# Who begins the transfer of the carried rows: ScalarE's queue in place of SyncE's

## The chip, the core and the metric

The kernel runs on one NeuronCore of a Trainium2 chip. The time is that of the device, in microseconds, for one execution of the whole program, and the median over several runs is compared. The names of the engines are those of the profile: PE is TensorE's matmul, PEld its weight load, DVE is VectorE, ACT is ScalarE, POOL is GpSimd and SP is SyncE, which only begins transfers. A `q` behind a name (SPq, ACTq) means the engine's instruction queue, which waits and begins transfers and in which the engine itself does no arithmetic.

## The reference

The input x has 32 batches of 512 channels by 1024 nodes, and adj is a 512 by 512 matrix. Layer 0 is a graph attention over the nodes, layer 1 a linear map with adj * adj, each behind a layer norm and a relu, and each added to x:

```
h = max(layernorm(x), 0)
q = wq . h ; k = wk . h                      # one number a node
scores[m, n] = leaky(q[n] + k[m], 0.01)
x = x + relu(adj @ (h @ softmax(scores).T) + bm)
h = max(layernorm(x), 0)
x = x + (adj * adj).T @ h + bias
```

## The kernel before

All is float32. The 1024 by 1024 scores are never formed. The leaky function has two slopes, so exp(score) is one product of exponentials where q[n] + k[m] is positive and another where it isn't. If the nodes are sorted by q, each output node needs one sum over an upper part of the sorted list and one over a lower part. So a batch goes through these steps, each a small function of the kernel:

- `load`, `stats`, `norm`, `slopes`, `relu` (layer 0): x comes in, ACT and DVE normalise it. `scores` (PE, then an ACT copy at L380 and a small transfer at L381 on ACT's queue) and `row` (L386, also on ACT's queue) spread q over all partitions.
- `rank` (DVE) and `lower` (ACT, L433) count for each node how many q are smaller. `value` (PE, L474) multiplies h with adj; `spread` (ACT, L481) copies each result out of its bank of PSUM; `scatter` (POOL, L487) writes the rows, sorted, into a table in DRAM (`td`).
- `fetch` (SP, L503) brings the sorted table back in three tiles `vs` of three blocks. `weights` (ACT, L510 to L515) makes the exponentials; `later` (DVE, L523 and L527) and `totals` prepare the weights and denominators; `stationary` (POOL, L546) multiplies masks with weights.
- `scan` and `sums` make the running sums over the nine blocks, once from each end. `scan` i multiplies block 8 - i into the upper 64 rows of a bank and block i into the lower 64 rows. `sums` i copies the bank out to a tile `t` (ACT, L574), puts the denominators beside it (ACT, L578) and has SP write both halves into the table (L580, L581).
- The sum so far has to enter the next block. In each block of 128 rows, row 0 or row 64 is kept free for it, so `sums` i carries the last sums, one row of 512 numbers for each direction, into the tiles `vs` that `scan` i + 1 reads. In batches 5 to 27 the rows go from `t` by two transfers of 2 KB (L576, L577); in the first five and last four batches ACT copies them straight from PSUM (L572, L573). The ninth block has nothing to carry.
- `gather` (POOL, L586) fetches for each node its sums, `excess`, `divide`, `weigh` (ACT, L611) and `combine` (DVE, L615) mix them, `turn` (PE and DVE, L622 and L626) transposes and adds to x.
- Layer 1: norm again, then seven products in place of eight on half-sized blocks. `seed` has ACT put the bias into banks (L648), `propagate` (PE, L657) multiplies, `mix` (DVE, L644) makes sums of blocks of h, `finish` (DVE, L670 and L674) adds to x, and `store` (SP, L701) writes out.

The order of all these steps, over several batches that are in work at once, is written out by hand in a long string, `ORDER`; every step is put into the queues of its engines in that order. There is no scheduler at run time: each engine goes through its own queue in order, and a waiting instruction holds up all that stands behind it in the same queue. `tp` has two buffers for `t`, `vsp` five for `vs`, and PSUM has eight banks that all steps share. Each transfer that SP or ACT begins counts on one of eight completion counters, taken in turn; before a transfer may use its counter, the one before on that counter must have landed.

Of the kernel before, what the change touches and what calls it, by code (L numbers as in the profile page):

```python
# [160 lines left out]
def kernel(  # L161
# [32 lines left out]
    nc = tc.nc  # L194
    B, C, N = x.shape
# [6 lines left out]
    HP = P // 2  # L202
# [364 lines left out]
    def sums(s, i):  # L567
        p = s.pt.pop(i)
        ha, hb = NB - 1 - i, i
        t = tp.tile([P, W], F32, tag="t", name=f"t_{s.b}_{i}")  # L570
        if i < NB - 1 and not LO <= s.b < B - HI:
            nc.scalar.copy(s.vs[ha - 1][0:1, 0:C], p[0:1, :])  # L572
            nc.scalar.copy(s.vs[hb + 1][HP : HP + 1, 0:C], p[HP : HP + 1, :])  # L573
        nc.scalar.copy(t[:, 0:C], p)  # L574
        if i < NB - 1 and LO <= s.b < B - HI:
            nc.sync.dma_start(s.vs[ha - 1][0:1, 0:C], t[0:1, 0:C])  # L576
            nc.sync.dma_start(s.vs[hb + 1][HP : HP + 1, 0:C], t[HP : HP + 1, 0:C])  # L577
        nc.scalar.copy(t[:, C:W], s.den[:, i : i + 1].broadcast_to([P, W - C]))  # L578
        td = tds[s.b % TABLES].rearrange("(s k) w -> s k w", k=4)
        nc.sync.dma_start(td[ts(ha, HP), 0, :], t[0:HP, :])  # L580
        nc.sync.dma_start(td[ts(hb, HP), 2, :], t[HP:P, :])  # L581
# [130 lines left out]
    for b in range(B):  # L712
        s = Batch()
# [8 lines left out]
        for f, count in (  # L722
            (rank, NN), (lower, NN), (value, NN), (spread, NN), (scatter, NN),
            (to_rows, 2), (scan, NB), (sums, NB), (gather, NN), (weigh, NN),
        ):
            plan(s, f, f.__name__, count=count)
# [30 lines left out]
    for code in ORDER.split():  # L757
        for k in range(0, len(code), 2):
# [3 lines left out]
            s, t = args[0], len(steps)  # L762
# [31 lines left out]
```

## Time and profile before

| | |
|---|---|
| median of 3 runs | 2300.36 us (2294.92 to 2301.21) |
| the profiled execution's own time | 2299.28 us |
| its span, first to last instruction | 2297.6 us |
| mean granted PE clock | 0.992 |
| busy: PE, DVE, ACT, POOL | 2225.3, 1735.6, 1703.1, 704.9 us |
| transfers begun at L576 and L577 | 184 and 184, on SP's queue, from 375.7 to 1974.8 us |
| one issue on SP, median | 539 ns at L576, 582 ns at L577 |
| one issue on ACT, median | 502 ns at L381, 341 ns at L386 |
| the two copies, mean | 581 ns at L574 (128 by 512), 207 ns (median) at L578 (128 by 16) |

All of it is one execution, recorded by the hardware. The busy time of an engine is the sum of its instructions; issues on a queue aren't counted in it. A line of the timeline has the start in us from the span's beginning, the length in us, the engine and the line of the kernel, the operation, what it writes and reads, the sizes and the count of instructions merged; in brackets at the end stand the idle time of the engine before it and what ended that. A line of the waits has who waited, for whom, the us in total, how often, and the longest.

### The profile page before, as it was taken

The numbers are of one execution on the slowest core, as the hardware profiler recorded it, in microseconds if no ns is written. First come the engines' busy times: TensorE is split into PE (matmuls) and PEld (weight loads), VectorE is DVE, ScalarE is ACT, GpSimd is POOL, SyncE is SP. The second block draws the span as 40 slices with busy tenths as digits, with TensorE's granted clock in tenths as the row PEclk, the third lists the DMA queues.
The fourth block names the chain that finished last, engine by engine and source line by source line (L and its number), as shares of the span: only waits on it lengthen the run. The fifth ranks groups of instructions, "written<-read, shape, count | busy, mean of one in ns | idle before, by whom it ended". The sixth has DMA issues, their size and how long they took to land. (4 is left out here: it accounts for less than half of the span.)

```text
span 2297.6 us, 28803 instructions
## 1 busy us (share of the span) xinstructions
PE 2225.3 (97%) x7344; PEld 954.0 (42%) x7344; DVE 1735.6 (76%) x4876; ACT 1703.1 (74%) x3269; POOL 704.9 (31%) x979
## 2 busy tenths in 40 slices
PE   6999999999999999999999999999999999999987
PEld 3434434344444444444444444444443444444343
DVE  6878878777877877777877877877777878778462
ACT  4698698777677877677877777877777876888752
POOL 2345223233232333232333232333222333234210
PEclk9999999999999999999999999999999999999998
DMA  6697887787888888888888888888888888788951
GB/s 234 225 341 258 310 290 294 276 298 266 314 284 303 299 314 282 291 281 314 295 316 290 300 275 304 309 302 294 300 275 293 301 310 277 283 283 314 368 220 73
DMA packets 217717, 657.77 MB, mean 286 GB/s; under 512 B 39376, under 2 KB 39504, under 8 KB 217552
## 3 DMA queue, kind: packets, MB, share of 16 engines
q1 hardware_dynamic: 153760, 362.16, 45.7%
q0 software_dynamic: 57344, 276.86, 31.4%
q10 hardware_dynamic: 6448, 16.92, 2.6%
q8 instruction: 59, 0.97, 0.2%
q14 instruction: 106, 0.87, 0.1%
HBM read 438.05 MB, written 217.01 MB: 285 GB/s over the span
## 5 line engine op out<-in xcount | busy, mean ns | idle before, releaser
L474 PE MATMUL pv<-wmT,x 128*128 128x512 f32 x2048 | 919.2, 598 | 0.7 <-ACT x L366 0.6
L474 PEld LDWEIGHTS pv<-wmT,x 128*128 128x128 f32 x2048 | 378.5, 190 | 496.5 <-issue 440.2
L487 POOL DMA_INDIRECT td<-v,idx x256 | 261.4, 1021 | 525.6 <-DVE junk L417 218.5
L657 PE MATMUL pg<-h,wsq 128*128 128x512 f32 x896 | 416.5, 599 | 5.2 <-DVE y L674 3.7
L615 DVE SCALAR_TENSOR_TENSOR g<-g,cf 128x512 f32<-128x512 f32 x512 | 365.9, 750 | 9.1 <-ACT g L611 6.5
L586 POOL DMA_INDIRECT g<-td,idg x256 | 245.0, 957 | 275.0 <-DVE y L626 87.2
L562 PE MATMUL sc<-vs,sm 128*64 128x512 f32 x1024 | 298.2, 615 | 18.7 <-DMA vs<-t 11.8
L433 ACT ACTIVATE junk<-qrow,qk 128x1024 uint8<-128x1024 f32 x256 | 293.6, 1147 | 27.7 <-DMA qrow<-qd 24.0
L546 POOL TENSOR_TENSOR sm<-mask_a,wc 128x192 f32<-128x192 f32 x96 | 65.9, 686 | 674.5 <-PE sc L562 445.6
L657 PEld LDWEIGHTS pg<-h,wsq 128*128 128x128 f32 x896 | 165.0, 190 | 236.2 <-issue 183.5
L481 ACT COPY v<-pv 128x512 f32<-128x512 f32 x256 | 145.6, 580 | 142.3 <-PE pv L474 70.3
L574 ACT COPY t<-sc 128x512 f32<-128x512 f32 x288 | 167.3, 581 | 111.3 <-PE sc L562 81.2
L670 DVE SCALAR_TENSOR_TENSOR y<-pg,bm_sb,y 128x512 f32<-128x512 f32 x224 | 166.8, 746 | 95.6 <-PE pg L657 95.5
L657 PE MATMUL pg<-mx,wmix 128*128 128x512 f32 x448 | 213.4, 600 | 1.3 <-ACT pg L648 1.3
L626 DVE SCALAR_TENSOR_TENSOR y<-tr,nbm,y 128x512 f32<-128x512 f32 x256 | 174.9, 746 | 31.7 <-PE tr L622 21.4
L366 ACT ACTIVATE x<-x,nmr,rstd 128x1024 f32<-128x1024 f32 x128 | 150.1, 1232 | 52.2 <-DVE nmr L359 51.6
L422 DVE TENSOR_SCALAR_CACHE_REDUCE junk<-qrow,qk,cnt 128x640 uint8<-128x640 f32 (+6 forms) x224 | 180.4, 805 | 8.2
L337 ACT ACTIVATE junk<-y,nm 128x1024 uint8<-128x1024 f32 x128 | 146.9, 1147 | 31.9 <-DVE nm L345 24.2
L417 DVE TENSOR_SCALAR_CACHE_REDUCE junk<-qrow,qk 128x384 uint8<-128x384 f32 (+6 forms) x224 | 165.8, 740 | 3.6 <-DMA qrow<-qd 1.7
L611 ACT ACTIVATE g<-g,cf 128x512 f32<-128x512 f32 x256 | 165.1, 711 | 4.4 <-DMA qd<-qr 2.2
L366 ACT ACTIVATE h<-y,nmr,rstd 128x1024 f32<-128x1024 f32 x128 | 151.6, 1230 | 4.0 <-DVE nmr L359 2.5
L562 PEld LDWEIGHTS sc<-vs,sm 128*64 128x64 f32 x1024 | 62.3, 135 | 200.7 <-issue 128.7
(135 smaller groups left out, 2535.6 us busy)
## 6 DMA issues: line engine op xcount, KB each, us to landing
vs<-td SPq DMA_DIRECT2D x96, 792.0 KB
td<-t SPq DMA_DIRECT2D x576, 132.0 KB
x<-in_x_dram SPq DMA_DIRECT2D x128, 512.0 KB
y<-in_x_dram SPq DMA_DIRECT2D x128, 512.0 KB
out_dram<-y SPq DMA_DIRECT2D x128, 512.0 KB
qrow<-qd ACTq DMA_DIRECT2D x32, 512.0 KB
vs<-t SPq DMA_DIRECT2D x368, 2.0 KB
td<-v,idx POOLq DMA_INDIRECT x256, 6.2
```

The lines of the kernel that those rows point to most:

```text
L366: nc.scalar.activation(h, s.x[c], AF.Relu, bias=s.nmr[:, c : c + 1], scale=s.rstd[:, c : c + 1])
L422: nc.vector.tensor_scalar(junk[:, j * P :], s.qrow[:, j * P :], qc, first, ALU.is_lt, ALU.add, accum_out=s.cnt[:, 1, j : j + 1],)
L433: nc.scalar.activation(junk, s.qrow, AF.Sign, bias=s.qk[:, 1, j : j + 1], accum_out=s.sgn[:, j : j + 1])
L474: nc.tensor.matmul(pv, s.h[c][:, ts(j, P)], wmT[:, c, :], start=(c == 0), stop=(c == NC - 1))
L487: i = nc.gpsimd.indirect_dma_start(tds[s.b % TABLES][:, :], bass.IndirectOffsetOnAxis(ap=s.idx[j // 4][:, j % 4 : j % 4 + 1], axis=0), v[: ...
L562: nc.tensor.matmul(p[ts(k, HP), :], m[:, k, :], s.vs[h][:, 0:C], start=True, stop=True)
L574: nc.scalar.copy(t[:, 0:C], p)
L586: nc.gpsimd.indirect_dma_start(s.g[:, j, :], None, tds[s.b % TABLES].rearrange("(s k) w -> s k w", k=3), bass.IndirectOffsetOnAxis(ap=s.id ...
L615: nc.vector.scalar_tensor_tensor(r, s.g[:, j, k * W : k * W + C], s.cf[:, k, j : j + 1], r, ALU.mult, ALU.add)
L626: nc.vector.scalar_tensor_tensor(xh, pt, nbm[:, o : o + 1], xh, ALU.max, ALU.add, accum_out=s.ys[:, i, o : o + 1])
L657: nc.tensor.matmul(s.pg[key], forms[m][:, r, ts(u, P)], data, start=(m == 2 and r == 0), stop=(r == 1), skip_group_check=True,)
L670: nc.vector.scalar_tensor_tensor(xh, s.pg[key, u], bm_sb[:, c + u : c + u + 1], xh, ALU.add, ALU.add)
```

## The change

The two transfers of the carried rows are begun by ACT, in its own queue between its two copies, in place of SP. What they move, and the rest of the kernel, stays as it is.

```diff
         nc.scalar.copy(t[:, 0:C], p)
         if i < NB - 1 and LO <= s.b < B - HI:
-            nc.sync.dma_start(s.vs[ha - 1][0:1, 0:C], t[0:1, 0:C])
-            nc.sync.dma_start(s.vs[hb + 1][HP : HP + 1, 0:C], t[HP : HP + 1, 0:C])
+            nc.scalar.dma_start(s.vs[ha - 1][0:1, 0:C], t[0:1, 0:C])
+            nc.scalar.dma_start(s.vs[hb + 1][HP : HP + 1, 0:C], t[HP : HP + 1, 0:C])
         nc.scalar.copy(t[:, C:W], s.den[:, i : i + 1].broadcast_to([P, W - C]))
```

## The prediction

> **What bounds the kernel now.** I read the busy table first, then busy time by stretch, then the waits of TensorE (PE) and ScalarE (ACT), and last the timeline of one batch, since a busy share says nothing about who waits for whom. The first line is the page's busy table; the second is the stretch 1001.80 to 1070.20 us, one batch of the steady part. Its columns after the stretch are the length, then busy us of PE, weight loads, VectorE (DVE), ACT and GpSimd, then the granted clock, the DMA share and GB/s.
>
> ```profile
> PE 2225.3 (97%) x7344; PEld 954.0 (42%) x7344; DVE 1735.6 (76%) x4876; ACT 1703.1 (74%) x3269; POOL 704.9 (31%) x979
> ...
> 1001.80:1070.20 68.40, 68.29 (x231) 29.72 (x230) 53.54 (x152) 52.02 (x103) 21.35 (x30) 1.00 0.84 299
> ```
>
> PE is busy for 68.29 of 68.40 us: in the steady part it is the bound, and nothing can be gained there. ACT has 68.40 - 52.02 = 16.4 us of idle time a batch. The next line is from PE's waits between 375 and 1974 us, the 23 batches whose carried rows go by DMA; the others are from SP's.
>
> ```profile
> PE sc L562 <- DMA vs<-t: 11.8, 12, 2.3
> ...
> SPq L577 <- DMA y<-in_x_dram: 21.8, 16, 2.4
> ...
> SPq L576 <- DMA qrow<-qd: 8.1, 12, 1.3
> ```
>
> PE waits 11.8 us for carried rows (15.4 with the waits of the weight loads, over the whole run); most of the 11.8 lies outside the steady part (5.1 before 660 us, 4.8 after 1754). PE is busy 1580.8 of these 1599 us, so 18.2 us is the most that any change here could gain.
>
> **What is moved, and its price on ACT.** 23 batches x 8 steps = 184 pairs, so 368 issues, go from SP's queue to ACT's. The built order of the changed kernel shows just that: 368 more instructions on ACT, each pair between the copy at L574 and the copy at L578, and nothing moved on PE or DVE. The first two lines are ACT's own timeline around such a step (the second is the copy that follows at once), the next two SP's pair for the same step, the last three an issue that ACT already makes after a copy.
>
> ```profile
> 1029.20 0.57 ACT L574 COPY t<-sc 128x512 f32<-128x512 f32 x1
> 1029.67 0.21 ACT L578 COPY t<-den 128x16 f32<-128x16 f32 x1
> ...
> 1029.80 0.53 SPq L576 DMA_DIRECT2D vs<-t  x1
> 1030.38 0.58 SPq L577 DMA_DIRECT2D vs<-t  x1
> ...
> 218.86 0.37 ACT L380 COPY qr<-pq 128x256 f32<-128x256 f32 x1 [1.05 <-PE pq L375]
> 219.26 0.50 ACTq L381 DMA_DIRECT2D qd<-qr  x1
> 219.81 0.57 ACT L572 COPY vs<-sc 1x512 f32<-1x512 f32 x1 [0.57 <-ACT qr L380]
> ```
>
> Today L578 starts 0.47 to 0.48 us after L574 starts, before that copy has ended. The last three lines show that an issue behind a copy costs ACT its whole length: it starts 0.03 us after the copy ends, takes 0.50, and the next copy starts 0.05 later. After the change, L578 starts at 0.58 (copy) + 0.03 + issue + 0.05 + issue + 0.05. With issues of 0.50 (ACT's row) that is 1.71, with SP's medians of 0.539 and 0.582 it is 1.83. Less 0.48, each step costs ACT 1.23 to 1.35 us; I take 1.30, since the form is SP's and the engine ACT's. In all 184 x 1.30 = 239 us, or 10.4 us a batch against 16.4 idle. So the total fits; what counts is where the idle time lies.
>
> [...]
>
> **Where ACT's lag meets slack.** From 1029.20 to 1064 us ACT has almost no idle time; all there is stands in the brackets of the first two lines here. Four of the batch's eight steps lie in it (1029.20, 1037.12, 1045.04, 1051.41).
>
> ```profile
> 1035.65 0.59 ACT L481 COPY v<-pv 128x512 f32<-128x512 f32 x1 [0.47 <-issue]
> 1037.12 0.59 ACT L574 COPY t<-sc 128x512 f32<-128x512 f32 x1 [0.45 <-PE sc L562]
> ...
> 1047.95 1.09 ACT L648 COPY pg<-bias_sb 128x512 f32<-128x512 f32 x2
> ...
> 1060.50 3.78 ACT L611 ACTIVATE g<-g,cf 128x512 f32<-128x512 f32 x6
> ...
> 1062.30 1.41 DVE L615 SCALAR_TENSOR_TENSOR g<-g,cf 128x512 f32<-128x512 f32 x2
> 1063.62 1.29 DVE L644 TENSOR_TENSOR mx<-h,mx 128x512 f32<-128x512 f32 x2
> ...
> 1064.50 0.19 PEld L657 LDWEIGHTS pg<-mx,wmix 128*128 128x128 f32 x1 [0.24 <-DVE mx L644]
> ```
>
> ACT's lag: 1.30 after 1029.20; minus 0.47 and 0.45 of idle leaves 0.38 at 1037.12; then 1.68, 2.98 after 1045.04, and 4.28 after 1051.41. Who waits for it:
> - The bias copies (L648) end at 1049.04; PE's product on them loads at 1051.09, slack 2.04 us (2.28 with the 0.24 us that a load stands ahead). Lag 2.98: PE late by 0.7.
> - The first of the six weighs ends at 1061.23, and the second of DVE's combines at L615 reads it at 1062.96: slack 1.73. DVE goes on to mx, and the weight load at 1064.50 follows mx's first half by 0.19, with 0.24 to spare. Lag 4.28 - 1.73 - 0.43 = 2.12 us late on PE, which includes the 0.7.
> - The table weights (L512, L515) have 2.76 us before DVE reads them at 1068.14, then 0.20 through GpSimd to the scan: 1.3 late, covered by the 2.12.
>
> ACT's next step, at 1069.61, stood idle 1.78 us for PE, so the remaining 2.16 shrink to 0.4. The steps at 1001, 1009, 1010 and 1020 us are followed by ACT idle times of 2.72 (for DVE's nmr, whose own slack is 1.94 against a lag of 1.7), 3.88 (L380, for PE) and 1.29 (for qrow): covered, cost nothing; without that cover each would cost its 1.30. SP, freed of 184 x 1.12 = 206 us of issues, is a gain for nobody on the path, as PE waits for none of its other transfers here.
>
> **The sum.** Steady part, 660 to 1754 us: 16 batches x 2.12 = 34 us (1.84 to 2.29 for a step of 1.23 to 1.35). The other 7 batches have tighter places (around 499 us PE reads a bias copy 0.05 us after it ends, DVE the table weights after 0.1), so between 2.1 and the whole 4.28 each; I take 3, 21 us. Against that, rows that start right behind the copy can save PE part of the 15.4 us; I take 5. Sum +50 us on the profiled execution's own 2299.3 us: 2349; the median of the runs shown lies 1.1 above it, so 2350.
>
> **Rivals.**
> - Faster: the rows no longer queue behind SP's other issues, so PE's waits for them go, and ACT's lag stays within its slack. For it: at 1012.75 us SP issued a pair 1.98 us after its copy had ended. It decides if a step costs ACT under (2.16 + 0.92) / 4 = 0.77 us, below which four steps fit in slack and idle time. Price 15.4 us: 2285. Against it: 0.50 us an issue.
> - No change: the 16.4 us of idle take up all, and the waits for rows stay or go by a few us: 2294 to 2306. Against it is the solid stretch of 35 us above.
> - Much slower: each DMA waits for the one eight places before it on the same of eight completion counters, and now ACT stands in that wait with all its work behind it. In the built order 168 of the 368 issues have such a wait, 75 of them for a transfer of SP's. SP's rows for L576 and L577 on DMAs other than these come to 38.4 us (21.8 and 8.1 are shown); if all fell on ACT where it has no slack: 2350 + 38 = 2388. Against it: in the steady batch that wait falls at 1014 us, where ACT idles until 1014.76.
>
> **Range and chances.** About 0.3%, 7 us, is what a measurement can tell from no change. Forecast 0.78, much slower 0.08, no change 0.07, faster 0.07; so slower 0.86. Low end: 16 x 1.84 = 29, nothing from the 7 other batches, less 15.4 for the rows: +14, 2314. High end: 16 x 2.29 + 7 x 4.28 = 67, plus 21.8 of waits for loads: +89, 2389, and 6 us for the rest of those waits: 2395.
>
> **What would show it.** Right: ACT's first copy of t and the L578 behind it 1.7 to 1.8 us apart; steady batches of about 70.5 us, with PE idle for "ACT pg L648" and "DVE mx L644"; ACT's waits for PE smaller. Wrong: an issue on ACT under 0.3 us, or L578 started during the issues; batches still 68.4 us; or PE waiting on rows as before while ACT stands in L577 for loads.

## The result and the profile after

The changed kernel takes 2375.93 us (median of 4 runs, 2371.12 to 2378.14) against 2300.78 for the kernel before: a ratio of 1.0326, 95% interval 1.0308 to 1.0345. It is 75 us slower, inside the range and 26 us above the forecast. The profiled execution took 2377.51 us, with a span of 2375.8.

The busy table of the changed kernel, and the stretch of 15 steady batches from one start of L380 to another (columns as in the prediction):

```profile
PE 2248.3 (95%) x7344; PEld 953.9 (40%) x7344; DVE 1732.6 (73%) x4876; ACT 1712.6 (72%) x3269; POOL 701.1 (30%) x979
...
674.30:1765.30 1091.00, 1044.22 (x3425) 445.01 (x3426) 802.36 (x2266) 787.04 (x1501) 320.02 (x452) 0.99 0.79 281
```

The same 15 batches of the kernel before:

```profile
669.50:1703.10 1033.60, 1030.23 (x3425) 444.81 (x3426) 805.62 (x2265) 780.58 (x1501) 321.06 (x452) 1.00 0.83 296
```

The instructions of PE are the same 3425, but the stretch is 57.4 us longer, 3.83 us a batch (72.73 against 68.91). The busy time of ACT hardly differs, since an issue isn't counted in it: a busy share doesn't show this cost. PE was idle 3.37 us in 15 batches before and 46.8 after, which is 43.4 of the 57.4 us. In the other 14.0 PE itself was busy for longer with the same work (1044.22 against 1030.23 us); where, is shown further down. Around one step, ACT's timeline now reads:

```profile
1052.32 0.57 ACT L574 COPY t<-sc 128x512 f32<-128x512 f32 x1
1052.92 0.50 ACTq L576 DMA_DIRECT2D vs<-t  x1
1053.46 0.60 ACTq L577 DMA_DIRECT2D vs<-t  x1
1054.11 0.20 ACT L578 COPY t<-den 128x16 f32<-128x16 f32 x1 [1.22 <-issue]
```

From L574 to L578 it is 1.79 us where it was 0.47 to 0.48, and ACT stands idle for 1.22 of them. Over the 184 steps with transfers the median is 1.80, against 0.48 before. PE's waits between 375 and 2040 us are now:

```profile
PE pg L657 <- DVE mx L644: 35.9, 17, 2.3
PE pg L657 <- ACT pg L648: 16.0, 22, 3.2
...
PE sc L562 <- DMA vs<-t: 5.4, 11, 0.8
...
PE sc L559 <- DMA vs<-t: 2.2, 6, 0.7
```

The waits for the rows went from 11.8 to 7.6 us. In their place PE waits for what DVE and ACT make, mx above all. What holds DVE up shows on its timeline, here with PE's line behind it:

```profile
1085.97 0.17 DVE L455 TENSOR_SCALAR rk<-sgn 128x8 f32<-128x8 f32 x1 [4.72 <-ACT junk L433]
...
1089.10 1.40 DVE L615 SCALAR_TENSOR_TENSOR g<-g,cf 128x512 f32<-128x512 f32 x2
1090.43 1.28 DVE L644 TENSOR_TENSOR mx<-h,mx 128x512 f32<-128x512 f32 x2
...
1091.16 1.98 PE L657 MATMUL pg<-mx,wmix 128*128 128x512 f32 x4 [2.11 <-DVE mx L644]
```

And what stands there in the kernel before, ACT's last sign count first, which the prediction didn't look at:

```profile
1058.49 0.19 ACT L433 ACTIVATION_READ_ACCUMULATOR junk<-qrow,qk 128x1 f32 x1
...
1058.71 0.17 DVE L455 TENSOR_SCALAR rk<-sgn 128x8 f32<-128x8 f32 x1 [1.42 <-ACT junk L433]
...
1061.69 0.69 DVE L674 TENSOR_TENSOR y<-pg,y 128x512 f32<-128x512 f32 x1 [0.44 <-PE pg L657]
```

L455 begins `from_rows`, 13 small DVE instructions that turn the sign counts of ACT (L433) into places in the table. DVE was already waiting for ACT there, 1.42 us; now it waits 4.72, and the combines and mx stand behind it in DVE's queue.

Behind the wait for mx, some of PE's matmuls are also slower. Two batches of the changed kernel differ in this, the second of them the one just shown; the rows are PE's timeline behind the wait, and the stretch of 4.20 us from its end on (columns as above, with the granted clock third from the end):

```profile
945.56 3.41 PE L657 MATMUL pg<-mx,wmix 128*128 128x512 f32 x4 [2.11 <-DVE mx L644]
...
950.89 1.08 PE L562 MATMUL sc<-vs,sm 128*64 128x512 f32 x4
...
1094.79 1.08 PE L562 MATMUL sc<-vs,sm 128*64 128x512 f32 x4
...
945.50:949.70 4.20, 4.14 (x6) 1.83 (x7) 3.82 (x8) 3.73 (x12) 0.00 (x0) 0.59 0.20 83
1091.10:1095.30 4.20, 4.14 (x12) 1.66 (x13) 4.09 (x10) 3.72 (x12) 0.00 (x0) 1.00 0.19 76
```

Behind equal waits of 2.11 us, the granted clock was 0.59 in one batch and 1.00 in the other, and the same eight matmuls took 5.33 us to the next scan in place of 3.63, 1.7 more. That happened in five of the 15 batches, 8.5 us in all, and in none of the same 15 before, where PE hardly waits. The other 5.5 us weren't followed one by one; the first matmul behind each such wait takes 0.70 us in place of 0.59.

### The profile page after: what moved, and what is told of

It reads as the page before. It is cut to its first block, busy times and chain, and to the rows that moved or that the text cites. A ratio compares the mean times of both kernels' runs of the same rounds, so it can differ in the third digit from the quotient of the medians.

```text
span 2375.8 us, 28613 instructions
## 1 busy us (share of the span) xinstructions
PE 2248.3 (95%) x7344; PEld 953.9 (40%) x7344; DVE 1732.6 (73%) x4876; ACT 1712.6 (72%) x3269; POOL 701.1 (30%) x979
## 5 line engine op out<-in xcount | busy, mean ns | idle before, releaser
L433 ACT ACTIVATE junk<-qrow,qk 128x1024 uint8<-128x1024 f32 x256 | 293.3, 1146 | 27.7 <-DMA qrow<-qd 21.2
L562 PE MATMUL sc<-vs,sm 128*64 128x512 f32 x1024 | 298.1, 616 | 13.9 <-POOL sm L546 6.1
L657 PE MATMUL pg<-mx,wmix 128*128 128x512 f32 x448 | 222.6, 621 | 40.9 <-DVE mx L644 35.9
L578 ACT COPY t<-den 128x16 f32<-128x16 f32 x288 | 59.0, 205 | 236.5 <-issue 231.3
L481 ACT COPY v<-pv 128x512 f32<-128x512 f32 x256 | 144.3, 574 | 101.6 <-PE pv L474 69.4
L574 ACT COPY t<-sc 128x512 f32<-128x512 f32 x288 | 166.5, 578 | 70.3 <-PE sc L562 57.9
```

The costliest lines, as they stand in the source:

```text
L433: nc.scalar.activation(junk, s.qrow, AF.Sign, bias=s.qk[:, 1, j : j + 1], accum_out=s.sgn[:, j : j + 1])
L562: nc.tensor.matmul(p[ts(k, HP), :], m[:, k, :], s.vs[h][:, 0:C], start=True, stop=True)
L657: nc.tensor.matmul(s.pg[key], forms[m][:, r, ts(u, P)], data, start=(m == 2 and r == 0), stop=(r == 1), skip_group_check=True,)
```

## The experiments

The theory behind the forecast, A, is that ACT's added time counts only in the stretch from 1029 to 1064 us of a batch, in which ACT has almost no idle time. Its rivals: B, that it counts wherever it falls; C, that the transfers on ACT's queue and their waits matter, not the time.

**Only the steps in the solid stretch, and only the others.**

```diff
-            nc.scalar.dma_start(s.vs[ha - 1][0:1, 0:C], t[0:1, 0:C])
-            nc.scalar.dma_start(s.vs[hb + 1][HP : HP + 1, 0:C], t[HP : HP + 1, 0:C])
+            q = nc.scalar if 2 <= i <= 5 else nc.sync      # the second kernel: not 2 <= i <= 5
+            q.dma_start(s.vs[ha - 1][0:1, 0:C], t[0:1, 0:C])
+            q.dma_start(s.vs[hb + 1][HP : HP + 1, 0:C], t[HP : HP + 1, 0:C])
```

> Only the rows of steps 2 to 5, which fall into ACT's solid stretch, are begun by ACT; those of steps 0, 1, 6 and 7 stay with SP. Theory A (ACT's lag in the solid stretch, 4 steps of 1.31 us with 0.92 us of idle between them, makes PE late through DVE): nearly the whole loss stays, 2358 to 2378 us. Theory B (the loss is ACT's added time wherever it falls, or its waits for other transfers, in proportion to the number of issues): half the loss, about 2338 us.

> The other half: only the rows of steps 0, 1, 6 and 7, behind which ACT stands idle for PE or DVE in the steady batches, are begun by ACT. Theory A: little is lost, 2298 to 2315 us, and what is lost lies in the batches before 670 and after 1700 us. Theory B: half the loss, about 2338 us.

Each kernel moves 184 of the 368 issues. The first measured 2382.56 us against 2306.92 for the kernel before on the same chip, a ratio of 1.0333 (1.0306 to 1.036): the whole loss. The second measured 2300.20 us, 0.997 (0.996 to 0.9981): slightly faster than before. DVE's wait at L455 in the steady batches goes with it. In the first kernel:

```profile
DVE rk L455 <- ACT junk L433: 66.5, 14, 4.9
```

and in the second, where it was 19.8 us in the kernel before:

```profile
DVE rk L455 <- ACT junk L433: 19.7, 14, 1.4
```

Theory B is out: the same number of issues costs all or nothing, by where they stand. The first kernel lies 5 us above the top of what A gave, but this chip is slower by 6 us with the kernel before as well (2306.92 against 2300.78); its ratio agrees with the change's own 1.0326.

**One of the two rows.** L576 on ACT, L577 on SP:

```diff
             nc.scalar.dma_start(s.vs[ha - 1][0:1, 0:C], t[0:1, 0:C])
-            nc.scalar.dma_start(s.vs[hb + 1][HP : HP + 1, 0:C], t[HP : HP + 1, 0:C])
+            nc.sync.dma_start(s.vs[hb + 1][HP : HP + 1, 0:C], t[HP : HP + 1, 0:C])
```

> One of the two rows (L576) is begun by ACT, the other (L577) by SP. A step then costs ACT 0.58 + 0.03 + 0.50 + 0.05 - 0.48 = 0.68 us. Theory A: the idle time in the stretch takes off a larger part, the lag is about 2.0 us in place of 4.3, and less than half of the loss is left: 2315 to 2332 us. Theory B: half, about 2338 us.

Measured: 2317.13 us, a ratio of 1.005 (1.0032 to 1.0069). The step's median, over the 184, is 1.17 us, 0.68 above the kernel before, as worked out. Half the issues cost 0.005 of 0.0326, under a sixth: so the loss isn't in proportion, as it should be if the idle times and slacks of the stretch swallow a fixed amount of lag first. The 15 steady batches are 70.2 us long on the mean, 1.3 above before.

**ACT's time without the transfers.** SP begins both rows as before; ACT gets two copies whose output nothing reads.

```diff
             nc.sync.dma_start(s.vs[hb + 1][HP : HP + 1, 0:C], t[HP : HP + 1, 0:C])
+            junk = wp.tile([P, N], U8, tag="junk2", name=f"junk4_{s.b}_{i}")
+            nc.scalar.copy(junk, bias_sb)
+            nc.scalar.copy(junk[:, 0:192], bias_sb[:, 0:192])
```

> SP begins both rows as before; ACT gets two copies of a constant into a scratch tile at the same place (1024 and 192 elements a partition, added work that nothing reads), about 1.3 us a step. Theory A (ACT's time alone): as slow as the change, 2360 to 2385 us. Theory C (the transfers on ACT's queue, their waits for completion counters, or when the rows land): as before the change, about 2300 us.

Its timeline on ACT:

```profile
1044.58 0.56 ACT L574 COPY t<-sc 128x512 f32<-128x512 f32 x1
1045.04 1.04 ACT L579 CAST junk<-bias_sb 128x1024 uint8<-128x1024 f32 x1
1046.12 0.35 ACT L580 CAST junk<-bias_sb 128x192 uint8<-128x192 f32 x1
1046.38 0.20 ACT L581 COPY t<-den 128x16 f32<-128x16 f32 x1
```

The den copy, here L581, starts 1.80 us after the first copy; over the 184 steps the median is 1.81, 0.01 more than in the changed kernel. Measured: 2390.90 us, 1.0359 (1.0332 to 1.0386). With no transfer moved, the loss is there; the interval overlaps that of the change. Theory C is out: 1.3 us of ACT's time at each step is enough.

**The wait at L455.** In batches 5 to 27 `from_rows` is put just before the next batch's `columns`, where DVE is idle; everything else is the changed kernel, and, as a control, the kernel before.

```diff
+    moved, held = [], []
+    for step in steps:
+        if step[2] is columns:
+            moved += held
+            held = []
+        if step[2] is from_rows and LO <= step[3][0].b < B - HI:
+            held.append(step)
+        else:
+            moved.append(step)
+    steps = moved + held
```

> As the changed kernel, but in batches 5 to 27 the step from_rows (13 small DVE instructions, the first of which waits at L455 for ACT's last sign count) stands later in the order, just before the next batch's columns, where DVE is idle. Theory D (the term that I left out: DVE waits at L455 for ACT in order, with the combines and mx queued behind it, so that ACT's whole lag reaches PE): the lag reaches PE through the weighs alone, with 1.73 us of slack, and some 1.7 us in each of 16 steady batches come back: about 27 us less than the changed kernel, a ratio of 1.018 to 1.024. Theory E (another path of the same length stands behind it, such as the table weights or the bias copies): 1.030 or more.

> The kernel before with the same later place of from_rows, as a control of the last run: PE has no idle time in the steady batches, so theories D and E both expect no change, a ratio of 0.997 to 1.003.

The first measured 2355.54 us, a ratio of 1.0217 (1.0191 to 1.0243); the control 2307.41, 0.9997 (0.9982 to 1.0012). So (1.0326 - 1.0217) x 2307, about 25 us of the loss, went by way of L455. A steady batch is 71.1 us long, 1.8 above the control's 69.3. PE's waits for mx are shorter, and none of the 15 batches has a group of slow matmuls, so the 25 us take in the 8.5 that these cost. What is late next is the step that the prediction had named: DVE's combines now wait for the weighs, and mx stands behind them.

```profile
1080.86 0.75 DVE L615 SCALAR_TENSOR_TENSOR g<-g,cf 128x512 f32<-128x512 f32 x1 [0.85 <-ACT g L611]
1081.95 0.82 DVE L615 SCALAR_TENSOR_TENSOR g<-g,cf 128x512 f32<-128x512 f32 x1 [0.34 <-ACT g L611]
1082.69 1.28 DVE L644 TENSOR_TENSOR mx<-h,mx 128x512 f32<-128x512 f32 x2
```

**The issues under a long instruction.** All rows are begun by ACT, but those of steps 2 to 5 only behind ACT's next instruction of 1.05 us or more:

```diff
+    held = []
+
+    def release():
+        for to, row in held:
+            nc.scalar.dma_start(to, row)
+        held.clear()
...
-            nc.scalar.dma_start(s.vs[ha - 1][0:1, 0:C], t[0:1, 0:C])
-            nc.scalar.dma_start(s.vs[hb + 1][HP : HP + 1, 0:C], t[HP : HP + 1, 0:C])
+            held.append((s.vs[ha - 1][0:1, 0:C], t[0:1, 0:C]))
+            held.append((s.vs[hb + 1][HP : HP + 1, 0:C], t[HP : HP + 1, 0:C]))
+            if not 2 <= i <= 5:
+                release()
```

`release()` is also called behind each ACT instruction of `stats`, `lower` and `relu`, and ahead of `scan` and `sums`, so that some rows come out beside a shorter one (those at 1061.34 us beside copies of 0.58 us).

> All rows are begun by ACT, but those of steps 2 to 5 only behind ACT's next long instruction (1.05 to 1.23 us) in its queue, by which time the copy that they read is done; nothing is left out. Theory F (what costs is that ACT stands idle behind the copy; an issue needs ACT's queue, not ACT, and runs while the long instruction does): the loss goes, 2295 to 2315 us at 2307 for the kernel before. Theory G (each issue takes time from the engine itself): four steps still cost 1.1 us each, about 2370 us.

Measured: 2323.03 us, 1.0072 (1.0045 to 1.0098), against 1.0326 with the issues right behind the copy. Its timeline on ACT (L587, L593, L338 and L576 are the copy, the den copy, the next square and the two issues):

```profile
1037.15 0.57 ACT L587 COPY t<-sc 128x512 f32<-128x512 f32 x1
1037.62 0.21 ACT L593 COPY t<-den 128x16 f32<-128x16 f32 x1
1037.72 1.15 ACT L338 ACTIVATE junk<-y,nm 128x1024 uint8<-128x1024 f32 x1
1037.76 1.21 ACTq L576 DMA_DIRECT2D vs<-t  x2
...
1039.07 1.15 ACT L338 ACTIVATE junk<-y,nm 128x1024 uint8<-128x1024 f32 x1
```

The issues run from 1037.76 to 1038.97 while the square runs from 1037.72 to 1038.87, and the next square starts at 1039.07. Theory G is out by 47 us. F is the one that fits, though the time came 8 us above the top of what it gave: what costs is the time in which the queue makes the issues and ACT, which stands behind them, has nothing to do. Whether an issue that doesn't read the copy could run beside the copy wasn't tried. The steady batches are 69.4 us long, 0.2 above the last section's control (69.3, on the same chip), so there the loss is almost gone. Most of what is left of it lies outside: against that control, the four batches before take 287.0 us in place of 282.6 and the four after them 293.0 in place of 282.6, with some 3 us of slow matmuls as above in these. PE's waits for rows, 10.9 us at L562's place and 9.2 in the control, explain little of it; the rest is open.

**A version that beats both.** The kernel with steps 0, 1, 6 and 7 on ACT, at 0.997, is the fastest here. With `from_rows` later as well:

> The rows of steps 0, 1, 6 and 7 begun by ACT, as in the run that did so alone (0.997), with from_rows later as well. If the last microseconds of ACT's lag still reached PE through L455 there, it is 2 to 5 us faster than that run; if not, the same, 0.997.

Measured: 2302.82 us, 0.9981 (0.9965 to 0.9997). The interval overlaps that of 0.997, so no gain on top is shown. In the profiled execution of the kernel at 0.997, PE's waits for rows between 375 and 2000 us fell from 11.8 to

```profile
PE sc L562 <- DMA vs<-t: 6.3, 9, 1.8
```

5.5 us less, near the 6.7 us of the medians. That the gain comes from there isn't shown: the profiled execution was the slowest of the ten, 2304.88 us, and PE's idle time in it, span less busy time, is 75.0 us against 72.3 before.

## Why the prediction was right, point by point

- **The price of a step.** 1.30 us was forecast and 1.32 measured (medians over the 184 steps, 1.80 and 0.48). The issues took 505 ns (L576) and 607 ns (L577) on ACT, medians.
- **Where it counts.** Four steps in the stretch carry the loss, the other four nothing: shown by the pair of runs, 1.0333 and 0.997.
- **Who waits.** The mechanism, ACT's lag through DVE's mx to PE, was right; the term for a steady batch was too small, 2.12 us against 3.83. The step that failed is the list of those who wait for ACT: it gave DVE's combines 1.73 us of slack behind the weighs and left out L455, which stands ahead of the same combines and had no slack at all (ACT's last sign count ends at 1058.68, L455 starts at 1058.71). By that row the 4.28 us of lag lose only the 0.44 us that DVE idles before L674 and the 0.43 of the weight load, which makes 3.4. With L455 out of the way, a batch lost 1.8 us, near the 2.12 of the prediction's own path. A second term was put at nothing: that PE runs slower behind its waits. The slow matmuls in five of the 15 batches make 8.5 us, 0.6 a batch. 3.4 and 0.6 are 4.0, 0.2 above the measured 3.83.
- **The batches outside the steady part.** 21 us were forecast. From the starts of L380, the four batches before 670 us take 292.0 in place of 286.5 us and the four after 1703 take 297.5 in place of 282.1: 20.9 us together, net of the rows that land earlier. The 5 us taken off for those was about the size (4.2 us less waiting), but it was not a further gain on top of the measured stretches. That 21 was met is in part luck: it was a choice between 2.1 and 4.28 us a batch, and slow matmuls, which these batches have as well (around 656 and 2029 us), weren't in it.
- **The sum again.** Steady part 57.4 (15 batches) in place of 34 (16), the rest 20.9 in place of 21 - 5: 78 us on the profiled execution, 2375.8 - 2297.6. The prediction's 2.29 for a step of 1.35 us should read 2.32 (4 x 1.35 - 0.92 - 2.16), which moves its high end by less than 1 us.
- **The rivals.** "Faster" holds for the half of the steps whose lag is covered, by 6.7 us and not 15.4. "Much slower", ACT standing in the wait for a counter: from copy to den copy the 184 steps took 254.6 us more than before, 1.38 on the mean against a median of 1.32, so such waits cost ACT some 0.06 x 184 = 11 us in all, not 38.

## What to carry to other kernels

Here a pair of issues that read what their engine had just written made that engine stand still, 1.22 us a step, until the write was done and the issues were made; put such issues where the engine idles anyway, or behind a long instruction that doesn't need it. A total of idle time says nothing about such a price: follow the added time instruction by instruction through the stretch without gaps, and list every reader of the late engine, also the small ones, since a wait of 0.17 us of work holds up all that is queued behind it. A reader that already waits for the engine, however shortly, has no slack. And a wait of the engine that bounds the kernel can cost more than its length: here 1.7 us of slower matmuls followed a wait of 2.11, in five of 15 batches.

## What the runs showed of the hardware

An issue in ACT's queue and an instruction on ACT overlap nearly in full: two issues of 1.21 us together ran beside one square of 1.15 us, and the next square started 1.35 us after it, where in the kernel before two such squares follow each other in 1.28 us (1029.77 to 1031.05).

Behind waits of TensorE of 2.11 to 2.30 us, the granted clock fell in five of 15 batches (0.59 over 4.20 us in one of them), and four or five matmuls took about 1.06 us in place of 0.59; behind as long waits in the other ten they took 0.59, but for the first, 0.70. In the kernel before, three matmuls behind waits of 0.77 and 1.82 us did so too (granted clock 0.79 from 470 to 478 us).
